# Seven operand tiles, a moved output and projections between feed-forward steps in a fused attention kernel

## The chip, the cores and the metric

The kernel runs on one core of one Trainium2 chip. The metric is device time in microseconds (us) of one execution. Three executions were timed, and one more was recorded by the hardware profiler. All data is 32-bit floating point.

The engines are called by the names of the profile: PE is the matrix engine (PEld its weight loads), DVE the vector engine, ACT the scalar engine, POOL the general-purpose engine, and SP the engine whose queue issues the DMA transfers. [...] SP is the only engine here that issues transfers[...].

## The reference

`x` has the shape 8 x 256 x 512: 8 sequences, 256 positions, 512 features. Cut to what matters:

```python
xn = layernorm(x)
# attention, 128 heads of 4 + 64 dimensions
c_q, c_kv = xn @ Wq_down, xn @ Wkv_down            # 512 -> 64 each
q_c, k_c, v_c = c_q @ Wq_up, c_kv @ Wk_up, c_kv @ Wv_up   # 128 heads x 4
q_r, k_r = xn @ Wq_rope, xn @ Wk_rope              # 128 heads x 64; one shared 64
scores = (q_c . k_c + q_r . k_r) / sqrt(68)        # per head, 256 x 256
s = (softmax(scores) @ v_c).reshape(8, 256, 512) @ Wo
# feed-forward network with low-rank additions
h = silu(lin1(xn)) * lin3(xn)                      # 512 -> 1376
g = silu(lin2(h))                                  # 1376 -> 512
out = x + s * g
```

## The kernel before

**First phase** (`first_phase`). The 2048 rows of `x` are taken in four blocks `tb` of 512. For each block the rows are normalized and turned (`norm`, `turn`), the narrow projections are made (`narrow`, `down`), and the feed-forward network runs in six steps `u` (`low` and `main`: 16 matmuls of 512 columns and their followers on ACT and DVE). `low_out` is called three times per block: it adds four quarters of `h` on POOL (L454 to L456) and makes four small matmuls. `gate_out` at the end makes `g` for four times 128 rows: three matmul groups `pf` each (L471), a silu on ACT into `gs` (two buffers, L475), and a transfer to DRAM (L476). The attention needs `xn` again, so `down` calls `sum_x`, which puts three quarters of `xnT` and four sums of quarters into the DRAM tensor `xs_d[tb]`.

**`between(step)`** is work of the attention that is laid into the first phase: step 1 in block 2 after `u` = 1, step 2 in block 3 after `u` = 1, step 3 before and step 4 after the last `low_out`, both ahead of the last `gate_out`. Step 2 makes the first keys, queries and values; steps 3 and 4 make projections 0 to 3.

**`Project(j)`** makes the rope queries of four heads for two sequences. It computes a 2 x 2 block product with seven products in place of eight: `first` makes four of them into four banks of PSUM with the operands `x` number 0, 4, 5 and 3, `second` the other three with 1, 6 and 2. One product is two calls of the matmul, which the chip runs as four matmuls. `take` copies banks to SBUF on ACT (tiles `e`, one buffer each), `join` adds them on POOL (L207 to L209), `end` adds on DVE. The weights come by `load_rope(j)` (512 KB, two buffers), the sums of the weights by `sum_w(j)` (for `j` below 32 made on POOL and stored, later loaded). There are 128 projections; the `x` operands change every 32, for the next two sequences: `load_xs` then loads all seven in one transfer of 1792 KB into one tile with one buffer.

**The main loop** goes over 64 blocks `n` = (sequence `b`, group `sg` of 16 heads). Each has two halves, and a half has four matmul quarters `r` twice (`one`, `two`). In a half the order is: `score` for `one` and `two` (96 matmuls, eight PSUM banks[...]), `maxima` on DVE, `exponentials` on ACT (these free the banks), the projection `j = 2n + half + 4` with its PSUM copies between the exponentials, and `transpose` on DVE (these free the `pr` tiles, six buffers). After the first half of block `n`, `weigh(n-1)` multiplies the weights of the block before with the values into one bank `av` (128 matmuls), scales it twice on ACT into `acc` tiles and adds on POOL. `normalize` divides on DVE into `outT[b]`, one of four chunks. Blocks 62 and 63 have no projection left.

**The outputs.** `finish(b, n)` multiplies `outT[b]` for 128 queries with `Wo` (four chunks, eight matmuls `po`, L702), multiplies by `g` (DVE, L705), adds `x` (POOL, L706) and stores (L707). `load_out` brings `g` and `x` in, with one buffer each. The dictionary `outs` lays twelve of the sixteen outputs into second halves of blocks; the last four follow the loop, in this order:

```python
normalize(last - 1)
load_out(B - 2, 0); finish(B - 2, 0)
load_out(B - 2, 1); finish(B - 2, 1)
load_out(B - 1, 0)
weigh(last); normalize(last)
finish(B - 1, 0)
load_out(B - 1, 1); finish(B - 1, 1)
```

Of the kernel before, what the change touches and what calls it, by code (L numbers as in the profile page):

```python
# [9 lines left out]
F32 = mybir.dt.float32  # L10
AF = mybir.ActivationFunctionType
ALU = mybir.AluOpType
# [3 lines left out]
P = 128  # L16
B, S, D = 8, 256, 512
# [16 lines left out]
def mla_ffn_gate_kernel(  # L34
# [60 lines left out]
    def bank(name):  # L95
        return ps_all.tile([P, 512], F32, tag="b", name=name)
# [44 lines left out]
    def sum_x(p, xnT):  # L141


        q = lambda k, e: xnT[:, 2 * k : 2 * k + 2, ds(e * S, S)]
        t = xsp.tile([P, 7, 2, S], F32, tag="xs", name=f"xt_{p}")
        nc.gpsimd.tensor_sub(t[:, 3], q(0, 1), q(0, 0))
        nc.gpsimd.tensor_sub(t[:, 4], q(1, 1), t[:, 3])
        nc.gpsimd.tensor_sub(t[:, 5], q(1, 1), q(0, 1))
        nc.gpsimd.tensor_sub(t[:, 6], q(1, 0), t[:, 4])
        for i, of in enumerate((q(0, 0), q(1, 0), q(1, 1))):  # L150
            nc.sync.dma_start(out=xs_d[p][:, i], in_=of)
        nc.sync.dma_start(out=xs_d[p][:, 3:7], in_=t[:, 3:7])

    def load_xs(p):
        if p < B // 2:
            xsums[p] = xsp.tile([P, 7, 2, S], F32, tag="xs", name=f"xs_{p}")
            nc.sync.dma_start(out=xsums[p], in_=xs_d[p])

    def product(bank_, w, x, first):

        for c in range(2):
            nc.tensor.matmul(  # L162
                bank_,
                w[:, c],
                x[:, c],
                start=first and c == 0,
                stop=c == 1,
                skip_group_check=True,
            )

    class Project:
# [21 lines left out]
        def first(self):  # L193

            for i, (w, x) in enumerate(
                ((self.a(0, 0), 0), (self.s[:, 1], 4), (self.s[:, 2], 5), (self.s[:, 0], 3))
            ):
                self.banks.append(bank(f"q{i}_{self.j}")[:, 0:S])
                product(self.banks[i], w, self.x[:, x], True)

        def take(self, i):
            nc.scalar.copy(self.e[i], self.banks[i])  # L202
# [8 lines left out]
        def second(self):  # L211

            for i, w, x in ((0, self.a(0, 1), 1), (2, self.a(1, 1), 6), (3, self.s[:, 3], 2)):
                product(self.banks[i], w, self.x[:, x], False)
            nc.scalar.copy(self.out(0, 0), self.split(self.banks[0]))

        def end(self):
# [62 lines left out]
    def first_phase(between):  # L280
# [15 lines left out]
        def load_x(tb):  # L296
            xts[tb] = []
            for n in range(4):
                t = f1.tile([P, D], F32, tag="xt", name=f"xt_{tb}_{n}", bufs=6)
                nc.sync.dma_start(out=t, in_=x[ds(tb * TB + n * P, P), :])  # L300
                xts[tb].append(t)
# [183 lines left out]
        for tb in range(NTB):  # L485
            more = tb + 1 < NTB
            for u in range(6):
                low(tb, u)
                main(tb, u)
                if u in (2, 4):  # L490
                    low_out(tb, u // 2 - 1)
                if u == 1 and more:
                    norm(tb + 1)
                if u == 1:
                    if tb + 2 < NTB:
                        load_x(tb + 2)
                    else:
                        between(tb + 3 - NTB)
            if more:
                turn(tb + 1)  # L500
                low_out(tb, 2)
                narrow(tb + 1)
                down(tb + 1)
            else:
                between(3)
                low_out(tb, 2)
                between(4)
            gate_out(tb)
        st.close()

    def set_up():
# [36 lines left out]
    def between(step):  # L548
        if step == 0:
            set_up()  # L550
        elif step == 1:
            load_act(0)
            load_act(1)
            for j in range(2):
                load_rope(j)
        elif step == 2:
            prepare(0, 0)
            prepare(1, 0)
            spread(0)
            values(0)  # L560
            values(1)
            place_values(0)
            sum_w(0)
            sum_w(1)
            load_xs(0)
        elif step == 3:
            for j in range(2):
                Project(j).all()
                load_rope(j + 2)
                sum_w(j + 2)  # L570
        else:
            for j in range(2, 4):
                Project(j).all()
                load_rope(j + 2)
                sum_w(j + 2)
            load_act(2)
            load_act(3)

# [65 lines left out]
            prs.pop((n, f, r)).rearrange("p h (k j) -> p h k j", j=32),  # L644
        )

    def weigh(n):


        b, sg = blocks[n]  # L650
        vpad = vpad_of.pop(n)
        av = bank(f"av_{n}")
        for half in range(2):
            pt = [pts.pop((n, half, r)) for r in range(4)]
            for k in range(8):
                for r in range(4):
                    nc.tensor.matmul(  # L657
                        av[32 * r : 32 * r + 32, ds(half * P, P)],
                        vpad[:, k, r, :],
                        pt[r][:, k].rearrange("p q i -> p (q i)"),  # L660
                        start=(k == 0),
                        stop=(k == 7),
                        skip_group_check=True,
                    )

        accs[n] = []
        for what in range(2):
            a = smp.tile([P, S], F32, tag=f"acc{what}{sg % 2}{b % 2}", name=f"acc{what}_{n}", bufs=1)
            side = (sg + what) % 2
            nc.scalar.activation(a, av[:, :S], AF.Copy, scale=sides_sb[:, side : side + 1])  # L670
            accs[n].append(a)
        if sg % 2:
            for one, two in zip(accs[n - 2], accs[n]):
                nc.gpsimd.tensor_add(one, one, two)

    def normalize(n):

        b, sg = blocks[n]
        x, y = accs.pop(n - 2)
        if sg == 1:  # L680
            outT[b] = op.tile([P, 4, S], F32, tag="outT", name=f"outT_{b}")
        rec = smp.tile([P, S], F32, tag="rec", name=f"rec_{n}", bufs=1)
        nc.vector.stream_shuffle(rec, y, [i ^ 4 for i in range(32)])
        nc.vector.reciprocal(rec, rec)
        nc.vector.scalar_tensor_tensor(
            outT[b][:, sg // 2, :], x, 1.0, rec, ALU.mult, ALU.mult
        )

    gxs = {}

    def load_out(b, n):
        g = op.tile([P, D], F32, tag="g", name=f"g_{b}_{n}", bufs=1)
        nc.sync.dma_start(out=g, in_=gates_d[2 * b + n])
        xr = op.tile([P, D], F32, tag="xr", name=f"xr_{b}_{n}", bufs=1)
        nc.sync.dma_start(out=xr, in_=x[ds(b * S + n * P, P), :])
        gxs[b, n] = g, xr

    def finish(b, n):
        g, xr = gxs.pop((b, n))
        po = bank(f"po_{b}_{n}")  # L700
        for c in range(KT):
            nc.tensor.matmul(  # L702
                po, outT[b][:, c, ds(n * P, P)], wo_sb[:, c, :], start=(c == 0), stop=(c == KT - 1)
            )
        nc.vector.tensor_mul(g, po, g)  # L705
        nc.gpsimd.tensor_add(g, g, xr)  # L706
        nc.sync.dma_start(out=out[ds(b * S + n * P, P), :], in_=g)  # L707

    last = len(blocks) - 1
    outs = {}  # L710
    for p in range(B // 2 - 1):
        for i in range(4):
            outs[16 * p + 17 + i] = 2 * p + i // 2, i % 2
    for n, (b, sg) in enumerate(blocks):
        for half in range(2):
            one, two = 2 * half, 2 * half + 1
# [38 lines left out]
            if half == 0:  # L755
                if n + 2 <= last and blocks[n + 2][1] % 2 == 0:
                    prepare(blocks[n + 2][0], blocks[n + 2][1] // 2)
                if n < last:
                    spread(n + 1)
                if n >= 2 and blocks[n - 2][1] % 2:  # L760
                    normalize(n - 2)
                if n >= 1:
                    weigh(n - 1)
                    place_values(n)
                if (sg == 7 and b % 2) or (sg == 0 and b and b % 2 == 0):
                    if b + 1 < B:
                        values(b + 1)
                if sg == 2 and b >= 2:
                    load_act(b + 2)
            elif n in outs:  # L770
                finish(*outs[n])
    normalize(last - 1)
    load_out(B - 2, 0)
    finish(B - 2, 0)
    load_out(B - 2, 1)
    finish(B - 2, 1)
    load_out(B - 1, 0)
    weigh(last)
    normalize(last)
    finish(B - 1, 0)  # L780
    load_out(B - 1, 1)
    finish(B - 1, 1)


# [64 lines left out]
```

## Time and profile before

| what | value |
|---|---|
| time of three executions, median (lowest to highest) | 2095.45 us (2091.44 to 2098.23) |
| the profiled execution's own time | 2094.74 us |
| its span, first to last instruction | 2093.0 us |
| mean granted PE clock | 0.992 |
| busy: PE, DVE, ACT, POOL | 2046.5, 1525.3, 1085.1, 719.2 us |
| first phase up to the last `pf` | 0 to 257.4 us |
| last transposes of the loop end | 2061.3 us |

The span is the time from the first to the last instruction of the profiled execution; its own time is 1.7 us more, and lies 0.7 us from the median of the three. A line of a timeline gives start, duration, engine, line of the kernel, operation, what it writes and reads, how many of them are merged, and in brackets how long the engine was idle before and what ended that. The waits view adds such idle times up. A table of stretches gives for each engine the busy time in a stretch, and the clock that PE was granted in it, 1.00 being full speed.

### The profile page before, as it was taken

How to read it: one execution, taken by the hardware profiler on the slowest of the kernel's cores; microseconds unless marked ns; L12 is line 12 of the kernel's file. 1: busy time of each engine (PE TensorE's matmuls, PEld its weight loads, DVE VectorE, ACT ScalarE, POOL GpSimd, SP SyncE). 2: the span in 40 equal slices, each digit the busy share in tenths (PEclk: the TensorE clock that was granted, in tenths of full speed). 3: DMA queues.
4: the chain of work that ended last, by engine and by line, in shares of the span. 5: the costliest groups of instructions: out<-in, count | busy, mean ns of one | idle time of the engine just before them, and what ended most of it. 6: DMA issues, size and time to landing. Idle time of an engine off the chain costs nothing.

```text
span 2093.0 us, 61071 instructions
## 1 busy us (share of the span) xinstructions
PE 2046.5 (98%) x25536; PEld 1671.2 (80%) x25536; DVE 1525.3 (73%) x2601; ACT 1085.1 (52%) x2989; POOL 719.2 (34%) x1037
## 2 busy tenths in 40 slices
PE   7999999999999999999999999999999999999996
PEld 3334688888888888888888888888888888888883
DVE  5332177878887777878786877788886867788895
ACT  2222265555655555555655545455555544565562
POOL 5335434555452322333233223332223233232321
PEclk9999999999999999999999999999999999999998
DMA  4233322222223132322123222222231232222201
GB/s 161 83 109 117 102 87 82 82 81 73 73 89 121 63 106 84 110 82 78 66 83 118 76 98 94 95 82 82 69 111 68 87 107 87 75 70 82 82 32 52
DMA packets 110262, 183.13 MB, mean 87 GB/s; under 512 B 8154, under 2 KB 80474, under 8 KB 108964
## 3 DMA queue, kind: packets, MB, share of 16 engines
q1 hardware_dynamic: 109988, 179.23, 24.6%
q8 instruction: 203, 3.33, 0.6%
q14 instruction: 71, 0.58, 0.1%
HBM read 145.12 MB, written 34.08 MB: 86 GB/s over the span
## 4 chain that ended last, share of the span: by engine, by line
PE 94%; DVE 2%; DMA 2%; POOL 1%; issue 0%; SPq 0%; ACT 0%; POOLq 0%; ACTq 0%; DVEq 0%
PE q L162 38%; PE sc L613 31%; PE av L657 11%; PE po L702 2%; PE px L428 2%; PE py L429 2%; PE pf L471 1%; PE px L414 1%; DMA xs<-xs_d 1%; DVE pt L642 1%; DVE nmx L626 1%; PE pm L381 1%; PE vps L261 1%; PE qk L234 1%; PE qk L235 1%; PE pp L381 1%
## 5 line engine op out<-in xcount | busy, mean ns | idle before, releaser
L632 ACT ACTIVATE pr<-sc,nmx 128x256 f32<-128x256 f32 x2048 | 818.7, 504 | 488.4 <-DVE nmx L626 486.9
L626 DVE TENSOR_REDUCE nmx<-sc 128x2 f32<-128x512 f32 x1024 | 635.6, 683 | 343.3 <-PE sc L613 311.9
L642 DVE STREAM_TRANSPOSE pt<-pr 128x512 f32<-128x512 f32 x1024 | 635.0, 678 | 0.0
L613 PE MATMUL sc<-act,qr 32*128 32x256 f32 x8192 | 493.8, 375 | 0.2 <-issue 0.2
L162 PE MATMUL q<-xs,ws 128*128 128x256 f32 x2048 | 486.7, 381 | 0.0
L207 POOL TENSOR_TENSOR e<-e,e 128x256 f32<-128x256 f32 x128 | 93.2, 728 | 1089.1 <-ACT e L202 568.9
L613 PEld LDWEIGHTS sc<-act,qr 32*128 32x128 f32 x8192 | 425.1, 185 | 23.1 <-issue 1.0
L162 PEld LDWEIGHTS q<-xs,ws 128*128 128x128 f32 x2048 | 391.4, 191 | 52.5 <-issue 0.2
L162 PE MATMUL q<-xs,w 128*128 128x256 f32 x1536 | 389.7, 390 | 10.3 <-DMA xs<-xs_d 7.5
L162 PEld LDWEIGHTS q<-xs,w 128*128 128x128 f32 x1536 | 292.3, 197 | 80.1 <-ACT pr L632 44.3
L613 PE MATMUL sc<-kc,qcm 32*128 32x256 f32 x4096 | 287.5, 388 | 2.6 <-ACT gs L475 2.5
L613 PEld LDWEIGHTS sc<-kc,qcm 32*128 32x128 f32 x4096 | 201.7, 185 | 53.1 <-issue 22.1
L657 PE MATMUL av<-pt,vpad 128*32 128x128 f32 x8192 | 236.8, 273 | 1.2 <-ACT pr L632 1.2
L657 PEld LDWEIGHTS av<-pt,vpad 128*32 128x32 f32 x8192 | 219.7, 110 | 22.9 <-POOL e L208 8.0
L202 ACT COPY e<-q 128x256 f32<-128x256 f32 x512 | 204.2, 400 | 29.4 <-PE q L162 20.8
L670 ACT ACTIVATE acc<-av,sides_sb 128x256 f32<-128x256 f32 x128 | 53.9, 472 | 242.3 <-PE av L657 242.3
L246 POOL TENSOR_TENSOR qcm<-qc,mask_sb 128x1024 f32<-128x1024 f32 x64 | 122.4, 1912 | 17.0 <-ACT qc L237 17.0
L432 DVE TENSOR_TENSOR hT<-gate,py 128x512 f32<-128x512 f32 (+1 forms) x48 | 32.5, 685 | 110.0 <-PE py L429 109.9
L209 POOL TENSOR_TENSOR qr<-e,e 128x256 f32<-128x256 f32 x128 | 93.8, 732 | 10.0
L208 POOL TENSOR_TENSOR e<-e,e 128x256 f32<-128x256 f32 x128 | 93.5, 730 | 10.0
L219 DVE TENSOR_TENSOR qr<-e,q 128x256 f32<-128x256 f32 x128 | 54.0, 422 | 44.5 <-POOL e L207 34.0
L276 POOL COPY vpad<-vall 32x128 f32<-32x128 f32 x256 | 76.8, 300 | 13.8 <-PE av L657 4.7
(94 smaller groups left out, 1125.4 us busy)
## 6 DMA issues: line engine op xcount, KB each, us to landing
w<-in_w_rope_dram SPq DMA_DIRECT2D x128, 512.0 KB
ws<-sums_d SPq DMA_DIRECT2D x96, 512.0 KB
sums_d<-ws SPq DMA_DIRECT2D x32, 512.0 KB
xs<-xs_d SPq DMA_DIRECT2D x4, 1792.0 KB
xt<-in_x_dram SPq DMA_DIRECT2D x16, 256.0 KB
xs_d<-xt SPq DMA_DIRECT2D x4, 1024.0 KB
gate_d<-gs SPq DMA_DIRECT2D x16, 256.0 KB
g<-gate_d SPq DMA_DIRECT2D x16, 256.0 KB
```

Source lines behind the costliest of these rows:

```text
L162: nc.tensor.matmul(bank_, w[:, c], x[:, c], start=first and c == 0, stop=c == 1, skip_group_check=True,)
L202: nc.scalar.copy(self.e[i], self.banks[i])
L207: nc.gpsimd.tensor_add(m6, m6, m1)
L208: nc.gpsimd.tensor_add(m7, m7, m6)
L209: nc.gpsimd.tensor_add(self.out(1, 1), self.split(m7), self.split(m5))
L246: nc.gpsimd.tensor_mul(qcm, qks[b, sg // 2][0].rearrange("p (q i) -> p q i", i=32).unsqueeze(2).to_broadcast([P, 8, 4, 32]), mask_sb[:, ds ...
L276: nc.gpsimd.tensor_copy(vpad[rows, :, :, 8 * t + 4 * (sg % 2) :][..., :4], valls[b][rows, :, sg])
L613: nc.tensor.matmul(sc[r][:, h, :], lhs.rearrange("p t i -> p (t i)"), rhs, start=(part == 0 and h == 0), stop=(part == 2), skip_group_chec ...
L626: nc.vector.tensor_reduce(nmx[:, r, :], scs[n, f][r], AX.X, ALU.max, negate=True)
L632: nc.scalar.activation(p[:, h, :], scs[n, f][r][:, h, :], AF.Exp, bias=nmxs[n, f][:, r, h : h + 1])
L642: nc.vector.transpose(pts[n, f // 2, r].rearrange("p k q i -> p q k i")[:, ds(2 * (f % 2), 2)], prs.pop((n, f, r)).rearrange("p h (k j) -> ...
L657: nc.tensor.matmul(av[32 * r : 32 * r + 32, ds(half * P, P)], vpad[:, k, r, :], pt[r][:, k].rearrange("p q i -> p (q i)"), start=(k == 0), ...
```

## The change

Four things change.

1. `sum_x` stores its three plain quarters first and each of the four sums as soon as it is made. `load_xs` loads the seven operands as seven transfers of 256 KB into seven tiles, in the order of their use.
2. In block 3 of the first phase a `between` step follows every `u`: step 2 after `u` = 0, step 3 (values) after `u` = 1, projections 0 to 3 after `u` = 2 to 5. The last `low_out` is followed directly by `gate_out`; then comes step 8, with two sums of weights and the loads of sequences 2 and 3.
3. The output (5, 1) moves from block 52 to block 62; `outT` gets three buffers.
4. After the loop, the last block is weighed and normalized by halves of its 256 queries, `put` makes three of four chunks of the last four outputs ahead, `give` does what follows the matmuls, and `load_out` uses `pr` tiles for three of four outputs.

```diff
-        t = xsp.tile([P, 7, 2, S], F32, tag="xs", name=f"xt_{p}")
-        nc.gpsimd.tensor_sub(t[:, 3], q(0, 1), q(0, 0))
...
-        nc.sync.dma_start(out=xs_d[p][:, 3:7], in_=t[:, 3:7])
+        for i, of in ((0, q(0, 0)), (1, q(1, 0)), (2, q(1, 1))):
             nc.sync.dma_start(out=xs_d[p][:, i], in_=of)
+        t = {i: xsp.tile([P, 2, S], F32, tag=f"x{i}", name=f"xt{i}_{p}") for i in range(3, 7)}
...
+            nc.gpsimd.tensor_sub(t[i], one, two)
+            nc.sync.dma_start(out=xs_d[p][:, i], in_=t[i])
 
     def load_xs(p):
         if p < B // 2:
-            xsums[p] = xsp.tile([P, 7, 2, S], F32, tag="xs", name=f"xs_{p}")
-            nc.sync.dma_start(out=xsums[p], in_=xs_d[p])
+            xsums[p] = {}
+            for i in (0, 4, 5, 3, 1, 6, 2):
+                xsums[p][i] = xsp.tile([P, 2, S], F32, tag=f"x{i}", name=f"x{i}_{p}")
+                nc.sync.dma_start(out=xsums[p][i], in_=xs_d[p][:, i])
@@ first_phase
-                if u == 1:
-                    if tb + 2 < NTB:
-                        load_x(tb + 2)
-                    else:
-                        between(tb + 3 - NTB)
+                if u == 1 and tb + 2 < NTB:
+                    load_x(tb + 2)
+                if tb == NTB - 2 and u == 1:
+                    between(1)
+                if not more:
+                    between(u + 2)
...
-                between(3)
                 low_out(tb, 2)
-                between(4)
             gate_out(tb)
+        between(8)
@@ between
         elif step == 2:
+            load_xs(0)
+            for j in range(2):
+                sum_w(j)
             prepare(0, 0)
             prepare(1, 0)
             spread(0)
+        elif step == 3:
             values(0)
             values(1)
             place_values(0)
-            sum_w(0)
-            sum_w(1)
-            load_xs(0)
-        elif step == 3:
-            for j in range(2):
-                Project(j).all()
-                load_rope(j + 2)
-                sum_w(j + 2)
+        elif step < 8:
+            Project(step - 4).all()
+            load_rope(step - 2)
+            if step < 6:
+                sum_w(step - 2)
         else:
-            for j in range(2, 4):
...
+            sum_w(4)
+            sum_w(5)
             load_act(2)
             load_act(3)
@@ weigh, gather, normalize: as before, but for one half or some columns
+    def weigh(n, half):
...
+    def gather(n, cols=ds(0, S)):
...
+        for what in (1, 0):
             side = (sg + what) % 2
+            nc.scalar.activation(
+                accs[n][what][:, cols], avs[n][:, cols], AF.Copy, scale=sides_sb[:, side : side + 1]
+            )
         if sg % 2:
+            for what in (1, 0):
+                one, two = accs[n - 2][what][:, cols], accs[n][what][:, cols]
                 nc.gpsimd.tensor_add(one, one, two)
 
-    def normalize(n):
+    def normalize(n, cols=ds(0, S)):
...
+            outT[b] = op.tile([P, 4, S], F32, tag="outT", name=f"outT_{b}", bufs=3)
@@ outputs
+    def load_out(b, n, spare=False):
+        g, xr = (
+            prp.tile([P, D], F32, tag="pr", name=f"{what}_{b}_{n}")
+            if spare
+            else op.tile([P, D], F32, tag=what, name=f"{what}_{b}_{n}", bufs=1)
+            for what in ("g", "xr")
+        )
...
+    def put(b, n, chunks):
+        if (b, n) not in pos:
+            pos[b, n] = bank(f"po_{b}_{n}")
+        for c in chunks:
+            nc.tensor.matmul(
...
+    def give(b, n):
         g, xr = gxs.pop((b, n))
+        nc.vector.tensor_mul(g, pos[b, n], g)
         nc.gpsimd.tensor_add(g, g, xr)
         nc.sync.dma_start(out=out[ds(b * S + n * P, P), :], in_=g)
...
+    outs[last - 1] = outs.pop(16 * (B // 2 - 2) + 20)
@@ after the loop
-    normalize(last - 1)
...
+    early, late = ds(0, P), ds(P, P)
+    weigh(last, 0)
+    gather(last, early)
+    for b in (B - 2, B - 1):
+        for i in range(2):
+            put(b, i, range(KT - 1))
+    weigh(last, 1)
+    gather(last, late)
+    load_out(B - 2, 0)
+    load_out(B - 2, 1, True)
+    load_out(B - 1, 0, True)
+    load_out(B - 1, 1, True)
+    normalize(last - 1)
+    normalize(last, early)
+    put(B - 2, 0, [KT - 1])
+    put(B - 2, 1, [KT - 1])
+    put(B - 1, 0, [KT - 1])
+    give(B - 2, 0)
+    give(B - 2, 1)
+    normalize(last, late)
+    put(B - 1, 1, [KT - 1])
+    give(B - 1, 0)
+    give(B - 1, 1)
```

## The prediction

> **What bounds the kernel now.** First the busy shares: PE is busy for 2046.5 of 2093.0 us, DVE for 73%, so time goes where PE waits, works slowly, or does work that another place would hide. The waits view for PE says where it stood:
>
> ```profile
> PE po L702 <- DVE outT L685: 9.8, 2, 7.8
> PE q L162 <- DMA xs<-xs_d: 7.5, 3, 3.0
> PE q L162 <- ACT e L202: 2.6, 2, 2.5
> PE sc L613 <- ACT gs L475: 2.5, 1, 2.5
> ```
>
> (total, times, longest). These are the four places that the change touches. PE's timeline shows more than the waits, for example where the third `xs` load is awaited:
>
> ```profile
> 1561.31 1.91 PE L613 MATMUL sc<-act,qr 32*128 32x256 f32 x32
> 1566.25 1.11 PE L162 MATMUL q<-xs,w 128*128 128x256 f32 x4 [3.04 <-DMA xs<-xs_d]
> 1567.19 4.44 PE L162 MATMUL q<-xs,ws 128*128 128x256 f32 x12
> ```
>
> Twelve matmuls take 4.44 us here and 2.75 elsewhere: after a wait PE runs slowly for a while. The table of stretches confirms it for the end of the kernel, where ten `po` matmuls fill each stretch:
>
> ```profile
> 2064.00:2071.00 7.00, 7.00 (x13) 2.72 (x14) 0.69 (x1) 0.00 (x0) 1.26 (x1) 0.64 0.10 37
> 2079.50:2084.10 4.60, 4.54 (x10) 1.80 (x10) 0.69 (x1) 0.00 (x0) 1.26 (x1) 1.00 0.18 71
> ```
>
> The third field from the end is the granted clock, 0.64 and 1.00. The first stretch follows an idle time of 7.79 us.
>
> **The x tiles.** A projection normally takes PE 6.05 us (28 matmuls, 0.215 each). Behind the three loads the time from its start to the next work is 7.81, 6.13 and 7.81 us, so slow clock costs 3.5 us beside the 7.5 of waiting: 11.0. With seven tiles the first load is released by the first product of the old projection. At the first of the three places that projection starts at 635.04, products take 0.86 us each, so loads are issued from 635.9 to 641.1; now the one load goes out at 641.39. The next projection could start at 646.75 (649.04 less 2.29), and needs its fourth tile only at 649.3, its last at 652.
>
> [...] The trace has a nearer row, four transfers of 256 KB from DRAM at the start:
>
> ```profile
> 0.75 1.82 SPq L300 DMA_DIRECT2D xt<-in_x_dram  x4
> 3.46 0.69 DVE L335 BATCH_NORM_STATS2 st<-xt 128x6 f32<-128x512 f32 x1 [3.46 <-DMA xt<-in_x_dram]
> 5.58 0.69 DVE L335 BATCH_NORM_STATS2 st<-xt 128x6 f32<-128x512 f32 x1 [0.42 <-DMA xt<-in_x_dram]
> ```
>
> The first lands 2.7 us after the issue, the third by 5.6, the fourth is not awaited at 6.46: they overlap, about 0.95 us each. So the last tile is there at 641.1 + 0.4 + 2.7 = 644.2, before the projection can start. I take the row: **-11.0** (between 0 and -11). SP issues six transfers more, 6 x 0.35 = 2.1 us per change of operands, mostly while it waited for PE anyway; behind them are the weights for the projection after next.
>
> In `sum_x` the last sum still ends when it did; its store was issued at 175.42, right after POOL's last sum, and the stores of the earlier sums go out while POOL works: 0.
>
> **The first phase.** Projections 0 to 2 take about 6.1 us each on PE, projection 3 10.75 (236.19 to 246.94): its bank copies wait for POOL, busy 10.3 us in that stretch with two sums of weights, `h` sums and joins. Between FFN steps each projection has 10.75 us (4.7 + 6.05); POOL's part, join 2.2, sum 2.9, `h` sums 3.8, fits even where a sum waits 4.0 us for its weights (222.23 issued, 226.25 begun). So -4.6. But the last `low_out` was covered by two projections and has now only `gate_out` behind it. From the start of projection 3, POOL ends the join at +6.65 (as in projection 0) and the `h` sums, 4.38 us, at +11.0; the first `pf` needs them for its third chunk, at +6.1 + 1.0 + 1.7 = +8.8. PE stands about 2.25 us.
>
> Does that also slow the clock? The trace has idle times of 2.03 and 2.20 us without a slow stretch, 2.29, 2.49, 2.51 and 3.04 with one. [...] by the rows even 2.29 us cost 1.75. This one lies between: half, 0.9. Sum: -4.6 + 2.25 + 0.9 = **-1.45**.
>
> **The start of the loop.**
>
> ```profile
> 259.34 4.67 SPq L476 DMA_DIRECT2D gate_d<-gs  x4
> 262.49 1.18 ACT L475 ACTIVATE gs<-pf 128x512 f32<-128x512 f32 x2 [9.60 <-DMA gate_d<-gs]
> 266.09 1.28 ACT L632 ACT_TABLE_LOAD   x1 [2.42 <-DMA gate_d<-gs]
> 266.12 4.88 DVE L626 TENSOR_REDUCE nmx<-sc 128x2 f32<-128x512 f32 x8 [18.33 <-DMA wo_sb<-in_w_o_dram]
> 268.27 1.14 PE L162 MATMUL q<-xs,w 128*128 128x256 f32 x4 [0.16 <-ACT pr L632]
> ```
>
> `pf` ends at 257.34, but the gates' stores stand on SP behind the loads for sequences 2 and 3, so the third silu waits for a buffer, the first maximum waits until the last store has landed (the new pools lie where the old ones were), and projection 4 starts 10.9 us after the last `pf`. With step 8 behind `gate_out` the stores go out at once: last silu 0.75 after `pf`, landing 2.4, table load 1.28, two exponentials and the bank 0.9, with gaps 5.4. Saved: **-5.5**. The maximum's line names `wo_sb`, whose transfers begin at 264.10. Nothing that a maximum reads or writes depends on `wo_sb`, and ACT's line at the same moment names the gate; I take the gate. If it is `wo_sb`, now behind the ten loads (5.3 us) on SP, 5 of these 5.5 stay lost. Also behind them: the weights of projection 6, due on POOL 19.4 us after projection 4 starts and now landing at about 15.6 + 4 = 19.6; slack to PE about 1 us, cost 0 to 2, taken 0.
>
> **The moved output.** In block 52 PE is dense; eight `po` matmuls, 1769.60 to 1773.13, go: **-3.5**. In block 62 they run where DVE sets the pace (nine and a half us per half, without gap from 2029.65 to 2061.27). There the product with `g` adds 0.69 on DVE, and a PSUM bank is held until it: the last quarter of the scores of block 63 waits until 2042.9, about 0.3 us more on DVE, and PE stands 2.3 us, again at the edge of a slow stretch (half of 1.8). Sum **+1.9**.
>
> **The end.** Now from 2053.3: three chunks, idle 7.79, slow `po`, `av`, chunks, idle 2.03, `po`, and twice about 6.2 us in which DVE waits for a `g` load behind one buffer; end at 2093.0. New, without the 1.9: PE weighs the first half from 2054.4 less 1.0 = 2053.4 (1.8), makes 12 chunks (24 x 0.43 = 10.3) to 2065.5, weighs the second half to 2067.4 (its transposes ended at 2061.3) and three last chunks to 2070. DVE has normalized block 62 (2.7) and the early half (1.45) by 2065.5. Then two products (0.69), the late half after them, to 2071.6, the last chunk 1.14, product 0.69, addition 1.26, and 3.44 from there to the end of the span as now (2089.56 to 2093.0): 2078.5. Four `g` and `x` loads wait for the last transposes and land by about 2065, under the chunks. **-14.5**.
>
> **Sum:** -11.0 - 1.45 - 5.5 - 3.5 + 1.9 - 14.5 = -34.05. Against the profiled 2094.74 that is 2060.7; the median shown is 0.7 above, so I say **2061**.
>
> **Rivals.**
> (a) The start keeps its wait, on `wo_sb` or the late weights: +5, 2066. For: the maximum's line. Against: ACT's line.
> (b) The tile loads run one by one[...]: +11, 2072. Against: the row above.
> (c) The end gains half, about -7: the chunks stand ahead of the second half's weighing in PE's order, and if they run at the 0.64 clock of today's stretch, or a bank or buffer is late: 2068. For: the idle times near 2.3. Against: PE has 14 us of gapless work.
> (d) Slower: a wait in the repeated block. Products read seven tiles with waits of their own, and `acc` is written in the other order; from 0.53 us per block, 64 x 0.53 = 34 eats everything; at 0.7 it is 2106. Against: operands are loaded once in 16 blocks, the scaling on ACT precedes the next maxima by 2.7 us of idle time.
> (e) A step does not do what it says (PE is not the bound in block 52, or the stall at `gate_out` is twice as long): within a few us of the forecast.
>
> **Chances.** Forecast with (e) 0.67, (a) 0.13, (b) 0.06, (c) 0.10, (d) 0.04. Range: 2054 (no slow stretches, and 4 for a stall that is shorter) to 2070, which takes in (a) and (c). Of this kernel 0.3%, some 6 us, can be told from no change. All but (d) and a mixture of (b), (c) and more are faster by over 0.3%: faster 0.95, within 0.02, slower 0.03.
>
> **What would show it.** Right: no wait of a projection for `xs`, projections of 6.1 us at the three changes and in the first phase; projection 4 about 5.4 us after the last `pf`; clock 1.00 from the last scores on; about 25 us from the last scores to the end. Wrong: a `pf` wait for POOL over 3 us, maxima that wait for `wo_sb` landing, waits of some tenths in every block, or a gap ahead of the second half's weighing.

## The result, and the profile after

The changed kernel takes 2063.98 us (median of four executions, 2060.74 to 2066.51), the one before 2096.09 us beside it (four executions, 2091.44 to 2098.23). The ratio is 0.9857, with a 95% interval from 0.9841 to 0.9873: 32 us less, where the sum had said 34. The profiled execution took 2066.51 us, its span is 2064.7 us, and PE was granted a mean clock of 0.997.

In the places of the change PE's waits (total, times, longest) are these now:

```profile
PE pf L477 <- POOL h L462: 2.2, 1, 2.2
PE po L727 <- DVE outT L703: 1.8, 1, 1.8
PE sc L618 <- DVE g L737: 1.5, 1, 1.5
```

Of the four waits shown of before three are gone, and the one for `outT` is down from 9.8 to 1.8. The waits for the `h` sums and for the product with `g` are new, and both had been foreseen.

PE's timeline at the third change of the `x` operands (start, duration, what ran):

```profile
1554.57 1.14 PE L168 MATMUL q<-x,w 128*128 128x256 f32 x4
1555.55 2.75 PE L168 MATMUL q<-x,ws 128*128 128x256 f32 x12
```

The projection has no idle time ahead of it, and its twelve matmuls take 2.75 us, no longer 4.44.

PE's timeline at the end of the first phase, and the table of stretches there and at the end of the kernel (busy time of PE, PEld, DVE, ACT and POOL, each with its count; then the granted clock, the share of the DMA engines, and GB/s):

```profile
243.41 1.98 PE L477 MATMUL pf<-w_sb,h 128*128 128x512 f32 x4
247.58 10.52 PE L477 MATMUL pf<-w_sb,h 128*128 128x512 f32 x20 [2.18 <-POOL h L462]
258.03 1.15 PE L618 MATMUL sc<-kc,qcm 32*128 32x256 f32 x16
```

```profile
244.15:247.56 3.41, 1.25 (x3) 0.19 (x1) 2.07 (x3) 0.03 (x1) 3.33 (x4) 1.00 0.17 59
247.56:250.97 3.41, 3.39 (x4) 1.51 (x5) 0.00 (x0) 0.60 (x1) 3.33 (x5) 0.50 0.01 2
2039.60:2053.90 14.30, 14.30 (x156) 7.85 (x153) 11.59 (x21) 5.19 (x15) 0.87 (x2) 1.00 0.35 113
```

`pf` stands for POOL's sums as foreseen, and for 3.4 us afterwards the clock is 0.50: four matmuls in the time of eight. At the end the clock is full, and PE is busy through the whole of the last stretch shown.

The start of the loop, from the timelines of SP, ACT, DVE and PE:

```profile
250.31 8.81 SPq L482 DMA_DIRECT2D gate_d<-gs  x4
258.18 0.60 ACT L481 ACTIVATE gs<-pf 128x512 f32<-128x512 f32 x1 [1.98 <-PE pf L477]
262.34 1.28 ACT L637 ACT_TABLE_LOAD   x1 [3.56 <-DMA gate_d<-gs]
262.61 4.88 DVE L631 TENSOR_REDUCE nmx<-sc 128x2 f32<-128x512 f32 x8 [16.25 <-DMA gate_d<-gs]
264.52 1.14 PE L168 MATMUL q<-x,w 128*128 128x256 f32 x4 [1.03 <-ACT pr L637]
```

The four stores go out as `gs` is made, from 250.31 on; before, SP issued the first at 259.34, though its `gs` stood at 250.32, after ten loads from 254.20 to 259.24. The maximum names the gate where it had named `wo_sb`, and projection 4 starts 6.49 us after the last `pf`. ACT's wait for the last store is 3.56 us (2.42 before).

PE's timeline of the end:

```profile
2039.63 1.96 PE L664 MATMUL av<-pt,vpad 128*32 128x128 f32 x64
2041.52 10.57 PE L727 MATMUL po<-wo_sb,outT 128*128 128x512 f32 x24
2052.02 1.95 PE L664 MATMUL av<-pt,vpad 128*32 128x128 f32 x64
2053.90 2.84 PE L727 MATMUL po<-wo_sb,outT 128*128 128x512 f32 x6
2058.53 1.13 PE L727 MATMUL po<-wo_sb,outT 128*128 128x512 f32 x2 [1.78 <-DVE outT L703]
```

One idle time of 1.78 us is left of 7.79 and 2.03, and no slow stretch.

Where the time went can be added up, since the loop repeats: the interval from the start of one block's weighing to the next block's is 26.9 or 27.8 us where nothing disturbs it (27.8 where `prepare` runs, as at the changes of `x`) and mostly 30.3 or 31.2 with an output in it, so that each place is one difference.

| place | before | after | measured | predicted |
|---|---|---|---|---|
| three changes of `x` operands | 31.80 + 30.02 + 32.54 | 27.78 + 27.78 + 27.77 | -11.0 | -11.0 |
| block 3 of the first phase, from its first `pm` to the first scores | 93.18 | 92.99 | -0.2 | -1.45 |
| first scores to projection 4 | 10.93 | 6.49 | -4.4 | -5.5 |
| block 52 without its output | 30.61 | 26.91 | -3.7 | -3.5 |
| block 62 with it | 18.47 | 20.28 | +1.8 | +1.9 |
| end, from block 62's weighing | 49.17 | 34.09 | -15.1 | -14.5 |
| sum | | | -32.6 | -34.05 |

The spans differ by 28.3 us. The other 4.3 are 0.9 before block 3, where profiles with the same code differ by 3 us, and some 3.5 us in other blocks: there the intervals exceed the smallest seen in any profile by about 2 us in sum before and 5.5 after. These pieces are taken up behind the experiments.

### The profile page after: what moved, and what is told of

It is laid out like the page before. It is cut to its first block, busy times and chain, and to the rows that moved or that the text cites. A ratio compares the mean times of both kernels' runs of the same rounds, so it can differ in the third digit from the quotient of the medians.

```text
span 2064.7 us, 61156 instructions
## 1 busy us (share of the span) xinstructions
PE 2037.4 (99%) x25536; PEld 1665.3 (81%) x25536; DVE 1526.4 (74%) x2605; ACT 1084.0 (52%) x2991; POOL 718.4 (35%) x1039
## 4 chain that ended last, share of the span: by engine, by line
PE 97%; DVE 1%; POOL 1%; DMA 0%; issue 0%; ACT 0%; POOLq 0%; SPq 0%; ACTq 0%; DVEq 0%
PE q L168 39%; PE sc L618 33%; PE av L664 11%; PE po L727 2%; PE px L434 2%; PE pf L477 2%; PE py L435 2%; PE px L420 1%; PE pm L387 1%; PE vps L267 1%; PE qk L240 1%; PE qk L241 1%; PE pp L387 1%; PE pm L449 1%; PE xpt L370 0%; DVE pt L647 0%
## 5 line engine op out<-in xcount | busy, mean ns | idle before, releaser
L168 PE MATMUL q<-x,ws 128*128 128x256 f32 x2048 | 483.9, 379 | 0.0
L168 PEld LDWEIGHTS q<-x,ws 128*128 128x128 f32 x2048 | 389.0, 190 | 51.4 <-issue 0.2
L168 PE MATMUL q<-x,w 128*128 128x256 f32 x1536 | 387.4, 388 | 1.0 <-ACT pr L637 1.0
L168 PEld LDWEIGHTS q<-x,w 128*128 128x128 f32 x1536 | 291.5, 196 | 70.6 <-ACT pr L637 40.9
L684 ACT ACTIVATE acc<-av,sides_sb 128x256 f32<-128x256 f32 (+1 forms) x130 | 54.2, 468 | 235.7 <-PE av L664 235.7
```

Of the source, the lines that this page charges most:

```text
L168: nc.tensor.matmul(bank_, w[:, c], x[:, c], start=first and c == 0, stop=c == 1, skip_group_check=True,)
```

## The experiments

Each kernel is the changed one with one edit, or with several where the text says so. The ones of one comparison ran on one chip beside the kernel before: u1 to u4 (2096.09 us before), then b1, x2, d1 and best (2094.43), then the other four (2092.78).

**u1: the `x` operands in one tile again.** The four sums of `sum_x` go back into one tile and one store as well.

```diff
...
-            for i in (0, 4, 5, 3, 1, 6, 2):
-                xsums[p][i] = xsp.tile([P, 2, S], F32, tag=f"x{i}", name=f"x{i}_{p}")
-                nc.sync.dma_start(out=xsums[p][i], in_=xs_d[p][:, i])
+            xsums[p] = xsp.tile([P, 7, 2, S], F32, tag="xs", name=f"xs_{p}")
+            nc.sync.dma_start(out=xsums[p], in_=xs_d[p])
...
```

> The changed kernel with the x operands back in one tile and one load of 1792 KB; all else as changed. Theory (the tiles give what the two traces show at the three changes of operands, 4.0 + 2.2 + 4.8 = 11.0 us, waits and slow clock together): 11 us slower than the changed kernel, so 21 us under the kernel before, and three waits of a projection for the load of 2.2 to 3.0 us each, two or more of them followed by a slow stretch of 3.4 us. Rival (the wait is then hidden elsewhere or the gain came with the other parts): less than 5 us slower than the changed kernel.

Measured: 2072.34 us (2065.68 to 2075.06), ratio 0.9883 [0.9863, 0.9903]; 8.4 over the changed kernel by the medians, but its own executions lie 9.4 apart. The trace is sharper: the three intervals are 31.81, 30.10 and 32.55, in sum 11.1 more, with 7.7 us of waits. PE's timeline at the third change:

```profile
1559.46 1.34 PE L162 MATMUL q<-xs,w 128*128 128x256 f32 x4 [3.04 <-DMA xs<-xs_d]
1560.59 4.25 PE L162 MATMUL q<-xs,ws 128*128 128x256 f32 x12
```

The wait and the slow twelve matmuls (4.25) are back. The tiles are worth 11 us by the intervals.

**x2: the order of the seven loads.** The prediction had said that the gain comes from the early release of the first tile. This edit puts first the tile that the old projection uses last, so that nothing can be loaded early.

```diff
-            for i in (0, 4, 5, 3, 1, 6, 2):
+            for i in (2, 0, 4, 5, 3, 1, 6):
```

> The changed kernel with the seven loads of the x operands in another order, number 2 first, then 0, 4, 5, 3, 1, 6. Number 2 is the one that the old projection releases last, so all seven are issued only after its end, as the one load was. Theory A (what helps is that a projection need only wait for a quarter of the operands, and pieces overlap): as the changed kernel within 1 us, no wait for x, since the second piece is there some 3 us after the issue and 5.4 us pass until the next projection. Theory B (what helps is the early release, five us before): waits of 1 to 3 us at each of the three changes of operands, mostly with a slow stretch, 6 to 11 us slower than the changed kernel.

Measured: 2061.73 us (2059.23 to 2063.05), ratio 0.9843 [0.9828, 0.9858], no wait for `x`, intervals 27.77, 27.78 and 27.92. SP's and PE's timelines at the first change:

```profile
634.21 3.40 SPq L163 DMA_DIRECT2D x<-xs_d  x7
...
639.50 1.14 PE L168 MATMUL q<-x,w 128*128 128x256 f32 x4
```

All seven go out after the old projection has ended (634.18), the last at about 637.6, and the next projection, which needs operand 6, loaded last, in its sixth product, 4.3 us (5 x 0.86) after its start, is not held. So the early release isn't needed. What counts is that a projection waits for one piece and not for the whole, and that the pieces overlap. At the first change of the changed kernel they are issued from 632.44 to 637.62 and land from 635.18 to 641.33, each 2.7 to 4.3 us after its issue; the one load of before landed 7.5 us after its own. In x2, one after another, at the 2.7 us that the first `xt` load of the span took, they would by estimate have ended at about 653. Which of the two counts for more, no run here separates.

**u2: the `between` steps of before.** Projections 0 and 1 ahead of the last `low_out`, 2 and 3 with the sums and loads behind it and ahead of `gate_out`.

```diff
-                if not more:
-                    between(u + 2)
...
             else:
+                between(3)
                 low_out(tb, 2)
+                between(4)
             gate_out(tb)
-        between(8)
...
```

> The changed kernel with the between steps where they stood before (projections 0 to 3 in a row at the end of the first phase, loads of sequences 2 and 3 ahead of the last gates). Theory: projection 4 starts 3.75 us later in the traces, 4.6 without the 0.9 that the changed profile lost before block 3, so 4 to 5 us slower than the changed kernel, 27.5 under the kernel before; projection 3 takes 10.7 us again and projection 4 starts 10.9 us after the last pf. Rival (the delay is caught up later, since DVE and ACT lag behind PE at the loop's start): within 1.5 us of the changed kernel.

Measured: 2068.45 us (2066.02 to 2073.98), ratio 0.9869 [0.985, 0.9888], 4.5 over the changed kernel. From block 3's first `pm` to projection 4 it takes 105.2 us in the trace, against 98.7 to 99.5 in runs with the new order. PE's timeline, with projection 3 and the first scores:

```profile
243.86 1.14 PE L168 MATMUL q<-x,w 128*128 128x256 f32 x4 [2.75 <-ACT e L208]
...
265.44 2.34 PE L619 MATMUL sc<-kc,qcm 32*128 32x256 f32 x11 [2.77 <-ACT gs L481]
```

Both old waits are back, and projection 4 is 11.3 us behind the last `pf` again. Steps and stores together are worth 4.5 us by the times and about 6 by the traces, not the 7 of the prediction.

**b1: the last `low_out` in the middle of projection 3.** It gives POOL the `h` sums ahead of the join, and PE three products of cover behind the narrow matmuls.

```diff
-                if not more:
+                if not more and u < 5:
                     between(u + 2)
...
             else:
+                pj = Project(3)
+                pj.first()
+                for i in (0, 2, 3, 1):
+                    pj.take(i)
                 low_out(tb, 2)
+                pj.join()
+                pj.second()
+                pj.end()
+                load_rope(5)
```

> The changed kernel with the last low_out laid into projection 3: after its first four products and their copies, ahead of its additions on POOL. Theory (the gates stand 2.2 us for the h sums on POOL, and a slow stretch follows that costs 1.7): no wait of pf for POOL, no slow stretch, last pf ends 20.7 us after projection 3 starts less 3.9, that is 17.8 in place of 21.7; 4 us faster than the changed kernel, 36 under the kernel before. Rival (POOL has the join still to do and ACT the low-rank part, and pf waits for these): less than 1.5 us faster.

Measured: 2057.98 us (2057.06 to 2061.18), ratio 0.983 [0.9814, 0.9845], the fastest of all. PE's timeline:

```profile
241.46 10.46 PE L477 MATMUL pf<-w_sb,h 128*128 128x512 f32 x24
...
259.03 1.14 PE L168 MATMUL q<-x,w 128*128 128x256 f32 x4 [1.72 <-ACT pr L645]
```

All 24 `pf` run in 10.46 us, without wait or slow stretch; from the start of projection 3 to the last `pf` it is 17.6 us where it was 21.7. Of these 4.1 us 0.7 is given back, since projection 4 now starts 7.2 us after the last `pf`: ACT loads its table 0.75 us after the first maximum has begun (256.84 and 256.09), where in the changed kernel it did so 0.27 us ahead of it (262.34 and 262.61). Why the order turned isn't shown.

**b3: what stands behind the last store on SP.** With b1's edit, step 8 goes behind the 32 loads of `wo_sb`, to see whether the transfers that follow the store delay its landing.

```diff
             gate_out(tb)
-        between(8)
         st.close()
...
+    between(8)
     prp = pool("pr", 6)
```

> The kernel with the last low_out inside projection 3, and step 8 (stores of two weight sums, loads of sequences 2 and 3) behind the 32 loads of Wo. Theory (what stands right behind the last gate's store on SP[...] delays its landing, for which the first maximum waits): from the end of the last silu to the first maximum 2.2 to 2.4 us in place of 3.5, projection 4 starts 1 us earlier after the last pf, 1 us faster than with low_out inside alone. Rival (the maximum waits for more than that store, or the store takes as long whatever follows): 3 us or more again, no faster.

Measured: 2060.82 us (2059.12 to 2061.41), ratio 0.9845 [0.983, 0.986]. ACT's and DVE's timelines:

```profile
253.96 0.60 ACT L481 ACTIVATE gs<-pf 128x512 f32<-128x512 f32 x1 [1.98 <-PE pf L477]
...
257.70 2.48 DVE L639 TENSOR_REDUCE nmx<-sc 128x2 f32<-128x512 f32 x4 [13.26 <-DMA wo_sb<-in_w_o_dram]
```

From the end of the silu to the first maximum it is 3.1 us, not the 2.2 to 2.4 expected. With the loads of `wo_sb` right behind it, as in the kernel before (2.45 us there), the store is still late; so what follows it on SP doesn't make it long. (The maximum's line names `wo_sb`, as it did before the change; it starts 0.4 us after the last part of the store has landed.)

The traces show what goes with the delay. A store's landing is recorded in sixteen parts. Before and in u2 the last part of this store lands at most 0.02 us after the fifteenth; in the other twelve profiles it lands 0.5 to 1.4 us after it. In these twelve, and not in those two, a transfer of 16 KB of the kind "instruction" runs while the store is on its way, as the DMA view of the changed kernel from 258.5 to 262.5 has it (packets, MB, share of the transfer engines):

```profile
q8 instruction: 1, 0.02, 2.3%
```

It runs there from 259.21 to 260.70; fifteen parts have landed by 260.81, the last lands at 262.19. In all twelve profiles the last part lands 1.44 to 1.55 us after such a transfer has ended. Without that lag, it would by estimate, from these times, be 2.4 to 2.7 us from the silu to the maximum in these twelve, where it is 2.45 before and 2.3 in u2. The store runs beside this transfer now that it goes out during the first scores; before, the transfer ran from 259.13 to 260.09, and the last store was issued at 263.69. No run moves one against the other on purpose, so what holds the last part isn't shown.

**u3: the output (5, 1) back in block 52.**

```diff
-    outs[last - 1] = outs.pop(16 * (B // 2 - 2) + 20)
```

> The changed kernel with output (5, 1) back in block 52. Theory: PE gets 3.6 us more in block 52, and the end loses the 1.55 us that PE stood for the product with g in block 63 and what followed of it: net 1.5 to 2.2 us slower than the changed kernel, 30 under the kernel before. Rival (the move gains nothing, since the bank and the product on DVE delay the end by as much as PE saves): within 0.7 us of the changed kernel, with the first half's weighing of block 63 earlier by 3 us or more after the last projection.

Measured: 2061.05 us (2060.17 to 2063.64), ratio 0.9839 [0.9823, 0.9856]: 2.9 faster than the changed kernel, against the expectation. In the trace the three intervals concerned are 30.35, 18.75 and 21.63 us against 26.91, 20.28 and 21.41, so the edit itself costs 2.1 us there; but the first 63 us of the span were 2.7 us shorter and the small idle times 1.9 us less in sum, neither of which the edit touches. The changed kernel had been timed on another occasion. So the comparison was made again, both sides on one chip, from a faster base (best2, below):

> The same but output (5, 1) in block 52, as before the change. Theory (the move is worth what the intervals between the weighings of the blocks 51, 61 and 62 show, 2.1 us, and 0.7 more with the product between the transposes): 2.8 us slower than with the output in block 62. Rival (the timed runs of the first such kernel, 2.9 us faster than the changed one, show something that the intervals do not): equal or faster.

Measured: 2061.43 us (2059.51 to 2062.97) against 2058.62: 2.8 slower; the intervals are 30.35, 18.47 and 16.76 against 27.30, 19.07 and 16.76. The ranges of the two still overlap, so it is the intervals, 2.5 us here and 2.1 in u3, that carry this: the move is worth 2 to 3 us.

**u4: the end of before** (cut to the calls). One weighing, one normalization, four outputs one after another.

```diff
+    normalize(last - 1)
+    load_out(B - 2, 0)
+    finish(B - 2, 0)
+    load_out(B - 2, 1)
+    finish(B - 2, 1)
+    load_out(B - 1, 0)
     weigh(last, 0)
-    gather(last, early)
...
     weigh(last, 1)
-    gather(last, late)
...
+    gather(last)
+    normalize(last)
+    finish(B - 1, 0)
+    load_out(B - 1, 1)
+    finish(B - 1, 1)
```

> The changed kernel with the end as before (whole block 63 weighed at once, four outputs one after another, one buffer each for g and x), output (5, 1) still in block 62. Theory: 14.6 us slower than the changed kernel, 17.5 under the kernel before, with three slow windows of 3.4 us and two waits of some 6 us for g again. Rival (most of it was the clock, and the move of output (5, 1) shortens the idle time): less than 10 us slower than the changed kernel.

Measured: 2075.85 us (2073.89 to 2079.09), ratio 0.9911 [0.9895, 0.9926], 11.9 over the changed kernel; in the trace 12.7. PE's timeline:

```profile
2049.69 6.30 PE L727 MATMUL po<-wo_sb,outT 128*128 128x512 f32 x10 [7.34 <-DVE outT L703]
2055.92 3.70 PE L664 MATMUL av<-pt,vpad 128*32 128x128 f32 x128
```

The idle time, the slow `po` behind it and DVE's two waits for `g` (12.3 us) are back. It is 2.4 us less than the kernel before lost. Of this the clock explains 0.8: the slow time that fell on PE's work was 5.2 us before (2063.94 to 2069.11) and is 3.5 here (2049.69 to 2053.23), at half speed. The two idle times are 0.6 us shorter.

**d1: the second half weighed two outputs earlier.** The prediction's rival (c) had put the cost of the end into the chunks ahead of the second weighing.

```diff
-    for b in (B - 2, B - 1):
-        for i in range(2):
-            put(b, i, range(KT - 1))
+    for i in range(2):
+        put(B - 2, i, range(KT - 1))
     weigh(last, 1)
...
     normalize(last, late)
+    put(B - 1, 0, range(KT - 1))
```

> The changed kernel with another order after the loop: the second half of block 63 is weighed after six of the twelve chunks, as soon as its transposes are done, the late half is normalized under the other six, and each output is given as soon as its last chunk stands. Theory (PE's work, 14 us without gap, bounds the end, and the wait of the last chunk for the late half, 1.8 us, goes): 1.5 us faster than the changed kernel; no wait of po for outT; about 23.5 us from the first half's weighing to the end in place of 25.1. Rival (the last product, addition and store are the bound, in a row on DVE, POOL and the transfer): less than 0.5 us.

Measured: 2062.79 us (2057.13 to 2065.3), ratio 0.9844 [0.9826, 0.9863]. PE's timeline:

```profile
2039.77 1.95 PE L664 MATMUL av<-pt,vpad 128*32 128x128 f32 x64
2041.65 5.42 PE L727 MATMUL po<-wo_sb,outT 128*128 128x512 f32 x12
2047.00 2.21 PE L664 MATMUL av<-pt,vpad 128*32 128x128 f32 x64
2049.13 8.85 PE L727 MATMUL po<-wo_sb,outT 128*128 128x512 f32 x20
```

No wait is left, and from the first half's weighing to the end it is 23.6 us, not 25.1. These 1.4 us don't show in the times: executions of this kernel differ by 8 us.

**Versions together.** `best` has b1, d1, the loads of step 8 ahead of its sums, and in block 62 the product with `g` between the transposes (`finish` moved into the second half's loop). `best2` has b1, b3, d1 and that product. `after_again` is the changed kernel once more, for the same chip.

```diff
-            sum_w(4)
-            sum_w(5)
             load_act(2)
             load_act(3)
+            sum_w(4)
+            sum_w(5)
...
                 transpose(n, one, r)
+            if half and n == last - 1:
+                finish(*outs.pop(n))
             for r in range(2):
```

> Four things together: the last low_out inside projection 3, the end with the early weighing, the loads of sequences 2 and 3 ahead of the stores of the two weight sums in step 8, and in block 62 the product with g of output (5, 1) between the transposes of its two quarters. Theory: -3.9 and -1.5 as for the parts alone, -1 since the last gate's store then lands in 2.4 us and not 3.6, -0.3 to -0.5 for a bank that is free 2.4 us earlier (no wait of scores for the product with g): 6.8 us faster than the changed kernel, 39 under the kernel before. Rival (the loop's start and block 62 are bound by DVE whatever the store and bank do): 5.4 us.

> The changed kernel once more, beside the next three on one chip. Its profile shows whether the pieces of idle time of 0.2 to 0.9 us on PE that wait for nothing visible, some 3 us in the blocks 46 to 57 of the first profile of it, stand at the same places. Theory (they are of the execution, not of the program): other places or sizes, the time within 2 us of 2064. Rival (they come with the changed program): the same blocks and sizes, 2064 to 2066.

> Low_out inside projection 3, step 8 behind the loads of Wo, the early weighing at the end, and in block 62 the product with g between the transposes. Theory: 3.9 + 1 + 1.5 + 0.7 = 7 us faster than the changed kernel on the same chip. Rival (the parts that gained in the profile are made up by later waits): less than 4 us.

| | median, us | range | ratio |
|---|---|---|---|
| changed kernel, again | 2062.11 | 2061.55 to 2067.48 | 0.986 [0.9837, 0.9882] |
| best | 2059.66 | 2056.81 to 2061.03 | 0.9833 [0.9818, 0.9849] |
| best2 | 2058.62 | 2055.72 to 2061.69 | 0.9836 [0.9818, 0.9854] |
| b1 alone | 2057.98 | 2057.06 to 2061.18 | 0.983 [0.9814, 0.9845] |

All three lie 2.5 to 6 us under the changed kernel and cannot be told from one another; best2 gave half of the 7 us that its parts add up to. In `best` the product between the transposes took 1.2 us off block 62 and about 1.0 came back in the end; the loads ahead of the sums left the first maximum 3.4 us behind the last silu. b1's edit is the one that pays.

**The small idle times.** PE's timeline of the changed kernel has pieces such as this, ended by "issue", that is by nothing that this view shows:

```profile
1718.01 1.34 PE L618 MATMUL sc<-act,qr 32*128 32x256 f32 x17 [0.58 <-issue]
```

They come at the same places of the program, not all of them in each execution, and with other sizes, up to 1.16 us: of 64 such idle times of 0.1 us or more between 70 and 2040 us in the fourteen profiles, 55 stand behind the weighings of blocks 15, 31, 46, 49, 50 and 53. The transfers of kind "instruction" on queue 8, 16 KB each and 203 in an execution, go with them: 60 of the 64 end 1.2 to 1.6 us after one of these transfers has ended (in the profiles of before and of the changed kernel all six, 1.40 to 1.60 us after it). Such transfers start 11 us apart in the median, so by estimate chance would bring two or three of the 64 so close. What PE waits for there isn't shown.

They sum to 0.45 us in the one profile of before, 2.2 and 2.1 in the two of the changed kernel, and 1.0 to 3.3 in the variants. The intervals as a whole exceed the smallest by more: about 2 us before, 5.5 and 4 in the changed kernel, 3.5 to 6.6 in the variants. Whether the changed program brings 2 us of this, or the one profile of before had little, isn't settled: rival (d), a cost in the repeated block, is ruled out at 34 us but not at 2.

**When a slow stretch follows.** In these traces all changes of the granted clock in one execution lie on marks 3.41 us apart: in the changed kernel the slow stretch behind `pf` lasts 3.41 us, and the full-speed one ahead of it 194.56, 57 times as much; before, the slow stretches inside the span last 3.41 us and, at the end, 10.24. So PE's idle time can be added up from mark to mark. Two places of u1 (the fields as in the tables of stretches above):

```profile
638.60:642.01 3.41, 1.14 (x24) 0.71 (x16) 3.30 (x6) 3.12 (x9) 0.00 (x0) 1.00 0.98 388
642.01:645.43 3.42, 3.33 (x8) 2.74 (x9) 3.27 (x7) 1.11 (x3) 0.00 (x0) 0.50 0.37 146
1099.40:1102.81 3.41, 1.77 (x8) 1.64 (x9) 3.41 (x7) 1.90 (x6) 0.00 (x0) 1.00 0.85 313
1102.81:1106.23 3.42, 3.42 (x17) 3.06 (x17) 2.03 (x4) 2.81 (x10) 0.00 (x0) 1.00 0.01 2
```

Each place has a wait for `xs`, of 2.36 and of 2.29 us. The first lies almost whole between two marks: PE is busy for 1.14 us, idle for 2.27, and the clock is halved at the next mark. The second lies across a mark, which leaves 1.64 us of idle time in the stretch shown and 0.65 in the one ahead of it, and the clock stays full. Counted over all fourteen profiles from 60 us to PE's last matmul, 17 stretches at full clock had 1.95 us of idle time or more, and half clock followed all 17; 8151 had 1.90 or less, and it followed none. Of the 17, five are of the kernel before, with 2.29 to 2.72 us, and one of the changed kernel, with 2.17. (In the first 60 us half clock also followed less, 1.63 us in the changed kernel and 0.52 in u1; the reason isn't shown.)

## Why the prediction was right, and where its terms were off

**What bounds the kernel** was read rightly: the four waits of PE and the slow stretches behind them made the difference, and each came back when its part was undone (u1, u2, u4).

**The x tiles**, -11.0: exact in size. The row of the four `xt` loads was the right one to take: no projection waits for a piece, in x2 neither. One step of the argument fell: it was not the early release. In x2 the first load went out 5.2 us later, counted from the start of the old projection, and the last 3.1 us later, and they were still in time, because they overlap and a projection waits only for the operand that it uses next.

**The first phase**, -1.45: it came to -0.2. The stall of `pf` was 2.18 us for the predicted 2.25, and projections 0 to 3 take 6.05 to 6.3 us on PE. The mis-sized term is "half, 0.9": the slow stretch came whole, 20 matmuls in 10.52 us where 8.7 are due. Seven profiles have this stall, and in all seven a stretch at 0.50 follows. The row with 2.20 us misled: that idle time lay across a mark (0.58 and 1.62 us), while 2.17 of the 2.18 us here lie between two marks. So "half" was a fair guess for a place not known against the marks: of 2.18 us, 1.95 fall between two marks in about half of all places (estimated as (3.41 - 2.18 + 2 x 0.23) / 3.41). That it came in seven of seven isn't explained.

**The start of the loop**, -5.5: it came to -4.4 in this profile and to about 5 in the repeats, where projection 4 starts 5.75 to 6.5 us after the last `pf`, predicted 5.4. That the gate and not `wo_sb` holds the maximum was right, and rival (a) wrong: no 5 us stayed. The mis-sized term is "landing 2.4": it is 2.8 to 3.6 on ACT, and the difference is the last sixteenth of the store, which lands 1.44 to 1.55 us after the end of a transfer of kind "instruction" that runs while the store is on its way (b3).

**The moved output**, -3.5 and +1.9: -3.7 and +1.8. That the +1.8 agrees is luck: half a slow stretch (0.9 us) stood in the prediction's 1.9, and none followed, since PE stood 1.55 us instead of 2.3; the product and the bank held for it cost 1.8 where 1.0 was foreseen. `best` took 1.2 of them away by giving the product an earlier place.

**The end**, -14.5: -15.1. From the first half's weighing to the end of the span it is 25.07 us; the prediction's 2053.4 and 2078.5 are 25.1 apart. Rival (c) was wrong: the chunks ran at full clock, with a gap of 1.78 us ahead of the very last one only.

**The sum** was 1.4 us too large by its terms; the rest between it and the profiled spans is the spread of small pieces and of the first 63 us. The two mis-sized terms, 0.9 us of slow clock and 1.1 of landing, both cost, with some 0.3 us more in the first phase; the end and the moved output gave 0.9 back, so that small errors hid each other in part.

## What to carry to other kernels

Where an operand that all later work reads arrived in one transfer behind one buffer, splitting it by the pieces that the consumer waits for removed the wait (7.7 us at three places in u1), even with no piece started earlier (x2). Price an idle time of the matrix engine with the slow stretch that can follow it, whole (1.7 to 1.8 us lost here), once it comes to about 2 us (1.95 us or more between two marks here), and look for independent matmuls to put under it: moving three products there took 3.4 us off the stage in the trace (b1), the further tuning of the end 1.4 (d1). Before believing a difference of 2 or 3 us, put both versions on one chip together and take the stage's own interval from the traces: u3 had the wrong sign until then.

## What the runs showed of the hardware

- The granted clock changed only on marks 3.41 us apart. From 60 us on, half clock followed each of 17 stretches from mark to mark in which PE was idle for 1.95 us or more, and none of 8151 with 1.90 or less (all fourteen profiles). One idle time of 2.29 us that lay across a mark (u1) gave no slow stretch; others of 2.17 to 2.51 between two marks did.
- Of 64 small idle times of PE that the profiles put down to "issue", 60 ended 1.2 to 1.6 us after the end of a 16 KB transfer of kind "instruction", of which 203 ran in an execution.
- Seven transfers of 256 KB from one queue, issued 0.5 us apart, were all in time within some 6 us of the last issue (x2); at the three changes of the changed kernel a piece landed 2.6 to 4.3 us after its issue, where the one of 1792 KB before landed 7.4 to 8.3 us after. One of 1792 KB made PE wait 7.7 us in sum at three places (u1).
- The same program differed from execution to execution by 2 to 9 us (b3: 2059.12 to 2061.41; u1: 2065.68 to 2075.06). The fourteen profiles reach their first `pf` between 67.0 and 70.6 us.
- From the end of the last silu to the first maximum, ahead of which the 256 KB store between them landed, it took 2.3 and 2.45 us in the two profiles in which no transfer of kind "instruction" ran beside the store, and 3.1 to 3.8 us in the twelve in which one did.
